# Two cross-attention layers on one core: the first layer's output projection, three of its products in two levels, others among the last weighted rows

## The chip, the cores and the metric

The kernel runs on one core of a Trainium2 chip. The metric is the device time of one execution in microseconds; the median of three runs of the kernel before is 636.7 us. All arithmetic is in 32-bit floating point.

## The reference

Two cross-attention layers, eight batches of 100 query rows with 1024 features, and a context of 1444 rows with 512 features for each batch. Cut to what matters:

```python
# layer 0: scale = 1024 ** -0.5
Q = x @ Wq + bq;  K = ctx @ Wk + bk;  V = ctx @ Wv + bv
weights = softmax(Q @ K.T * scale, axis=keys)
x = x + (weights @ V) @ Wo + bo
# layer 1: its own Wq, bq, Wk, bk, Wv, bv
w = softmax((x @ Wq + bq) @ (ctx @ Wk + bk).T * scale, axis=queries)
x = w @ (ctx @ Wv + bv) + x
out = layernorm(x) * gamma + beta
```

The first layer's softmax runs over the keys of a query, the second layer's over the queries of a key.

## The kernel before

**Weights multiplied first.** The kernel never builds Q, K or V. It multiplies Wq with Wk (`wqk0`, `wqk1`; tiles qk in the trace) and Wv with Wo (`wvo`; tile vo) for itself, and then works with the context's 512 features. For each layer `queries` makes gT = (x Wq Wk)^T for two groups of four batches, 400 columns each (tiles g0T, g1T). For each batch `scores` multiplies gT with the context (L846), the softmax follows, and `weighted_rows` multiplies the weights with the context again (L817, tile A). In the first layer the result is copied to A0T (L830), and `project0` multiplies it with vo and adds it to xT, which holds x transposed as eight blocks of 128 features by 800 columns.

**Seven products for eight.** Large products are done by Winograd's form of Strassen's scheme: four sums of quarters of the left factor (S1 to S4), four of the right (T1 to T4), and seven products X, Z, Y, X again, W, X again, Y again. X and Y are pairs of PSUM banks into which later products accumulate; after every product VectorE adds the bank to the quarters of the result that it belongs to (`add`), or ScalarE copies it (`put`). A bank cannot be accumulated into again before the last add has read it. `seven_products` (L202) does one level. `inner_product` (L255) does one product of the outer scheme by a second level of seven, with half the columns and half the blocks; it writes its own sums over its factors where it can, and yields after each of its seven products.

**Order.** TensorE's instructions stand in the program's order. The other engines' order is set by the framework's scheduler, except that VectorE calls made while `vector.in_order` is set keep their place in the program (L94 to L98; all such calls have line L96 in the profile, all matmuls of the schemes L163). Each engine works through its list in order, and waits at an instruction until what it needs is there.

**Buffers.** `unit` gives one of ten stream buffers, which hold context rows (c), context features (cT) and scratch; `bank` one of six PSUM banks, `bank2` one of two more. A buffer is taken again once its last reader is done. SP's DMA queue issues the context loads in order; GpSimd's queue loads Wv, gamma, beta and bv of the second layer.

**Around the change.** `alternated` runs a batch's 48 weighted-row matmuls (each shows as two instructions), alternating with the scores of the batch two further on; batches 6 and 7 of the first layer have no further scores and run alone. `project0` (L936) yields two `seven_products`, one for each half j of the 1024 output features; the rows r and groups g of the result are the quarters. X and Z of the first half need only the first group; they run between batches 6 and 7:

```python
        if b == B - 1:

            o0 = list(project0(AS, A0))
            next(o0[0])
            next(o0[0])
        run(alternated(b, 0, softmax0, A0[b // G][:, :, b % G * T : (b % G + 1) * T]))
```

After batch 7 come X of the second half, the rest of the first half, the rest of the second, and then the second layer's `queries` (products g_x, g_y, a second-level Z named g_z, g_x, a second-level W named g_w alternating with the last product of X). Meanwhile `key_bias_sums` (L570) makes the second layer's key bias: eight steps over 800 columns (L576, L578; tile kb), each adding to the last, then in `key_biases` a transpose and a reduction, and in `totals` a matmul (L546, tile c), three small VectorE operations, and `key_bias[1]`, which ScalarE adds to the scores when it evicts them (L858). That matmul stands just ahead of the second layer's first scores. Then follow g_y's last product, the scores of batch 1, and the weighted rows of batch 0.

Of the kernel before, what the change touches and what calls it, by code (L numbers as in the profile page):

```python
# [25 lines left out]
F32 = mybir.dt.float32  # L26
# [29 lines left out]
def two_layer_cross_attention(ctx: ExitStack, tc: tile.TileContext, a: dict, out: bass.AP):  # L56
# [23 lines left out]
    def row(name):  # L80
        return work.tile([P, E], F32, tag="row", name=name, bufs=3)
# [98 lines left out]
    def combine(to, x, y, op, engine=vector):  # L180
        for t, p, q in zip(to, x, y):
            engine.tensor_tensor(t, p, q, op)
# [69 lines left out]
        add(0, 1, Y)  # L252
        yield

    def inner_product(name, lhs, rhs, nb, width, t, put, add, right=None):  # L255

        h, w = nb // 2, width // 2

        def quarters(x, n):
            if len(x) == 1:
                return ([x[0][:, 2 * k : 2 * k + 2, c]] for c in halves(n) for k in range(2))
            return ([x[2 * k + i][:, c] for i in range(2)] for c in halves(n) for k in range(2))

        def room(x, t):
            t = t.rearrange("p (i n) -> p i n", i=2)
            return [t] if len(x) == 1 else [t[:, i, :] for i in range(2)]  # L270

        A11, A12, A21, A22 = quarters(lhs, nb * P)
        B11, B21, B12, B22 = quarters(rhs, width)
        S1, T1 = room(lhs, t[:, : 2 * h * P]), room(rhs, t[:, 2 * h * P : 2 * h * P + 2 * w])

        T2, T3, T4 = B11, B12, B21
        if right:
            T1, T2, T3, T4 = right
        combine(S1, A21, A22, ALU.add)
        combine(T1, B12, B11, ALU.subtract)  # L280
        combine(A21, A11, A21, ALU.subtract)
        combine(T3, B22, B12, ALU.subtract)

        def product(ps, left, right, fresh):
            half_product([ps], left, right, fresh, h, w)

        def steps():
            X = bank(f"{name}_x")
            product(X, A11, B11, True)
            put(0, 0, X)  # L290
            combine(T2, B22, T1, ALU.subtract)
            combine(A11, S1, A11, ALU.subtract)
            yield
            Z = bank2(f"{name}_z")
            product(Z, A12, B21, True)
            add(0, 0, Z)
            combine(T4, B21, T2, ALU.subtract)
            combine(A12, A12, A11, ALU.subtract)
            yield
            Y = bank(f"{name}_y")  # L300
            product(Y, S1, T1, True)
            put(1, 1, Y)
            yield
            product(X, A11, T2, False)
            put(0, 1, X)
            yield
            W = bank2(f"{name}_w")
            product(W, A22, T4, True)
            put(1, 0, W)
            yield  # L310
            product(Y, A12, B22, False)
            add(0, 1, Y)
            yield
            product(X, A21, T3, False)
            add(1, 1, X)
            add(1, 0, X)
            yield

        return steps()

    def halves(n):
        return slice(0, n // 2), slice(n // 2, n)
# [217 lines left out]
            tc.keep_in_program_order(ins)  # L540
        nc.vector.tensor_reduce(sums, t.rearrange("p (c q i) -> p c q i", q=P // QD, i=QD), AX.X, ALU.add)

    def totals(name, sums, n):

        ps = bank(name)[:, : n * P // QD]
        nc.tensor.matmul(ps, same, sums.rearrange("p c q -> p (c q)"), start=True, stop=True)  # L546
        own = small.tile([P, 2 * EC, P // QD], F32, tag="own", name=f"{name}_own", bufs=1)[:, :n, :]
        mask = quarter.unsqueeze(1).to_broadcast([P, n, P // QD])
        nc.vector.tensor_tensor(own, ps.rearrange("p (c q) -> p c q", q=P // QD), mask, ALU.mult)
        got = const.tile([P, n], F32, tag=name, name=name)  # L550
        nc.vector.tensor_reduce(got, own, AX.X, ALU.add)
        return got
# [17 lines left out]
    def key_bias_sums(name, wqbk):  # L570

        acc = work.tile([P, B * T + P - T], F32, tag="kb", name=name, bufs=1)
        nc.gpsimd.memset(acc[:, B * T :], 0.0)
        for k in range(EC):
            if k == 0:
                nc.vector.tensor_scalar(acc[:, : B * T], xT[:, k, :], wqbk[:, k : k + 1], None, ALU.mult)  # L576
            else:
                nc.vector.scalar_tensor_tensor(  # L578
                    acc[:, : B * T], xT[:, k, :], wqbk[:, k : k + 1], acc[:, : B * T], ALU.mult, ALU.add
                )  # L580
        return acc

    def key_biases(name, kb, bqbk):

        sums = quarter_sums(name)[:, :B, :]
        t = row(f"{name}_t").rearrange("p (b q j) -> p b q j", q=P // QD, j=QD)

        src = bass.AP(kb.tensor, kb.offset, [list(kb.ap[0]), [T, B], [QD, P // QD], [1, QD]])
        vector.transpose(t, src)
        vector.tensor_reduce(sums, t, AX.X, ALU.add)  # L590
        yield
        c = totals(name, sums, B)
        nc.vector.tensor_scalar(c, c, SCALE, bqbk, ALU.mult, ALU.add)
        yield c

    def queries(layer, w, u, between=None):
# [4 lines left out]
        H, nb, h = EC // 2, 2, GT // 2  # L601
        A11, A12, A21, A22 = ([w[:, k * H : (k + 1) * H, j * 256 : j * 256 + 256]] for j in range(2) for k in range(2))
        B11, B21, B12, B22 = ([xT[:, k * H : (k + 1) * H, g * GT : g * GT + GT]] for g in range(2) for k in range(2))
        S1, S2 = ([row(f"g{layer}_s{n}").rearrange("p (c l) -> p c l", c=H)] for n in (1, 2))
        T1, T2 = ([wide(f"g{layer}_t{n}")] for n in (1, 2))
        T3 = [work.tile([P, LC, GT], F32, tag="gT", name=f"g{layer}_t3", bufs=3)]
        dst = [work.tile([P, LC, GT], F32, tag="gT", name=f"g{layer}T_{g}", bufs=3) for g in range(2)]

        def put(r, g, banks):
            for j in range(2):  # L610
# [25 lines left out]
        def product(banks, lhs, rhs, fresh):  # L636
            half_product(banks, lhs, rhs, fresh, nb, GT)

        t = unit(f"g{layer}_t")

        def inner(n, lhs, rhs, put, add, right=None, at=0):
            return inner_product(f"g{layer}_{n}", lhs, rhs, nb, GT, t[:, at:], put, add, right)
# [3 lines left out]
            return [[t[:, n, :].rearrange("p (i t) -> p i t", i=2)] for n in range(4)]  # L646

        def steps():
            X = pair("x")
            product(X, A11, B11, True)  # L650
            put(0, 0, X)
            yield
            S3, S4 = A21, A12
            if layer == 0:
                Z = pair("z")
                product(Z, A12, B21, True)
            vector.in_order = layer == 0
            combine(S1, A21, A22, ALU.add)
            vector.in_order = True
            combine(T1, B12, B11, ALU.subtract)  # L660
            combine(S2, S1, A11, ALU.subtract)
            if layer == 0:
                combine(T2, B22, T1, ALU.subtract)
                vector.in_order = False
                yield
                vector.in_order = True
                add(0, 0, Z)
            combine(S3, A11, A21, ALU.subtract)
            if layer == 0:
                combine(T3, B22, B12, ALU.subtract)  # L670
            Y = pair("y")
            product(Y, S1, T1, True)
# [22 lines left out]
            V = half_steps(X, S3, T3, False, nb, GT)  # L695
            for n, _ in enumerate(inner("w", A22, T1, *parts(1, 0))):
                next(V)
                if layer == 0 and n == 1:
                    between()
                elif layer == 0 and n == 3:  # L700

                    add(0, 1, Y)
                    _, more = parts(0, 1)
                    Q = inner("q", S4, B22, more, more, four(T2[0]), 768)
# [62 lines left out]
    run(steps)  # L767
    wqbk0 = totals("wqbk0", sums_c, 2 * EC)
    nc.vector.tensor_tensor(out_bias, out_bias, wqbk0[:, EC:], ALU.add)
    kb0 = key_bias_sums("kb0", wqbk0[:, :EC])  # L770
    wqk1, (acc_c, acc_u) = next(qk1)
    c0 = next(got[0])
    for t in prob:
# [161 lines left out]

    def project0(AS, A0):  # L936

        Bs = [[A0[g][:, 2 * k + i, :] for i in range(2)] for g in range(2) for k in range(2)]
        t12, t4 = (work.tile([P, LC, GT], F32, tag="gT", name=f"o0_t{n}", bufs=3) for n in (12, 4))
        T_ = ([t12[:, i, :] for i in range(2)], [t12[:, 2 + i, :] for i in range(2)], Bs[2], chunks(t4, 2))  # L940
        for j, (A, S) in enumerate(AS):

            def add(r, g, banks, j=j):
                e = 4 * j + 2 * r
                add_to_queries([e, e + 1], g * GT, GT, banks)

            right = None if j else (lambda n: right_sums(Bs, T_, (n,)))
            yield seven_products(f"o0_{j}", A, Bs, S, T_, 2, GT, add, add, right=right)


    def softmax1(s, parts):
# [174 lines left out]
    first_transposed(batches[0], 0)  # L1126
    run(steps)
    for b in range(B):
        if b == B - 1:

            o0 = list(project0(AS, A0))
            next(o0[0])
            next(o0[0])
        run(alternated(b, 0, softmax0, A0[b // G][:, :, b % G * T : (b % G + 1) * T]))
        for e in range(2 * b, 2 * b + 2) if 2 * b < EC else ():
            add_out_bias(e)
        if b == 0:
# [3 lines left out]
        if b == 1:  # L1141
# [2 lines left out]
            vector.in_order = True  # L1144
            AS = value_sums(wvo)
            vector.in_order = False
    next(o0[1])
    for steps in o0:
        run(steps)

    gT[1], steps = queries(1, wqk1, u1)
    run(islice(steps, 5))
    kb1 = key_bias_sums("kb1", wqbk1)
    *_, key_bias[1] = key_biases("c1", kb1, bqbk1)
    vectors = [unit(f"vectors_{j}") for j in range(2)]
    gamma, beta = (t[:, :E] for t in vectors)
    bv1 = [t[:, E:] for t in vectors]
# [5 lines left out]
    nc.gpsimd.dma_start(out=wv1, in_=a["L1_xattn_Wv"].rearrange("(c p) e -> p c e", p=P))  # L1163


    run(first_scores(0, 1, softmax1))
    run(steps)
    run(first_scores(1, 1, softmax1))

# [44 lines left out]
```

## Time and profile before

| | |
|---|---|
| median of three runs | 636.7 us (636.08 to 637.99) |
| the profiled execution's own time | 636.75 us |
| its span | 635.0 us |
| TensorE busy, weight loads | 623.8 us, 530.7 us |
| VectorE, ScalarE, GpSimd busy | 472.4, 165.7, 98.7 us |
| granted clock | 0.997 mean |
| batches 6 and 7 with X and Z of the projection between | 322.9 to 350.6 us |
| rest of the projection, twelve products | 350.6 to 382.9 us |
| second layer's queries, up to its first scores | 382.9 to 414.4 us |
| first scores, g_y, second scores | 414.4 to 439.9 us |

An execution's time is its span and 1.75 us around it. A matmul's shown duration overlaps with the next one's start, so the distance from start to start is what it takes of the engine. On VectorE too the next instruction starts before the last one's shown end, unless it needs that result. A row of the timeline is start, duration, engine, line, operation, out<-in, shapes, count, and in brackets the idle time ahead of it and what ended it.

### The profile page before, as it was taken

Reading aid. Unit: us, or ns where it says so; the run is one execution under the profiler, and the core shown is the slowest. Engines: PE = TensorE matmul, PEld = TensorE weight load, DVE = VectorE, ACT = ScalarE, POOL = GpSimd, SP = SyncE. Lnnn points to the kernel's source line nnn. Section 1 sums busy time; section 2 is a strip of 40 time slices with the busy share of each in tenths; the row PEclk is TensorE's granted clock in tenths of the full one; section 3 lists DMA queues with packets and bytes.
Section 4 is the critical chain, followed back from the end, with each engine's and each line's share of the span. In section 5 each row is a group of like instructions: output and inputs, shape, how many; then the busy total and the mean of one; then the engine's idle time right before and its main releaser. Section 6 shows DMA issues by size and latency. Waiting matters only on the chain.

```text
span 635.0 us, 10448 instructions
## 1 busy us (share of the span) xinstructions
PE 623.8 (98%) x4112; PEld 530.7 (84%) x4112; DVE 472.4 (74%) x940; ACT 165.7 (26%) x377; POOL 98.7 (16%) x129
## 2 busy tenths in 40 slices
PE   9999999999999999999999999999999999999994
PEld 8886466688985999999998656756999999999992
DVE  2955779998884797676654789639777659898886
ACT  1522310105204244323230001113433240325301
POOL 2111200002300000000000001007211220544054
PEclk9999999999999999999999999999999999999998
DMA  8989997015779889998965206156899990699002
GB/s 270 298 166 295 307 333 242 1 47 103 154 272 387 277 299 310 334 300 310 310 220 186 91 0 232 48 192 189 284 303 303 320 313 26 196 322 339 30 18 87
DMA packets 51943, 138.32 MB, mean 218 GB/s; under 512 B 4339, under 2 KB 8691, under 8 KB 51895
## 3 DMA queue, kind: packets, MB, share of 16 engines
q1 hardware_dynamic: 46792, 120.85, 55.9%
q0 software_dynamic: 4704, 16.35, 11.3%
q8 instruction: 32, 0.52, 0.3%
q10 hardware_dynamic: 398, 0.47, 0.2%
q14 instruction: 17, 0.13, 0.1%
HBM read 123.36 MB, written 3.28 MB: 199 GB/s over the span
## 4 chain that ended last, share of the span: by engine, by line
PE 92%; DVE 3%; DMA 2%; issue 1%; POOL 1%; POOLq 0%; ACT 0%; DVEq 0%; SPq 0%
PE s L846 25%; PE A L817 25%; PE qk_x L163 7%; PE o_x L163 5%; PE g_x L163 4%; PE o_y L163 3%; PE qk_y L163 2%; PE qk_z L163 2%; PE vo_x L163 2%; DMA vo<-in_L_xattn_Wo 2%; PE g_y L163 2%; PE o_w L163 2%; PE o_z L163 2%; PE qk_w L163 1%; PE vo_y L163 1%; PE z L1045 1%
## 5 line engine op out<-in xcount | busy, mean ns | idle before, releaser
L817 PE MATMUL A<-w,c 120*128 120x100 f32 (+1 forms) x1536 | 247.7, 265 | 0.0
L817 PEld LDWEIGHTS A<-w,c 120*128 120x128 f32 (+1 forms) x1536 | 215.9, 190 | 0.8
L96 DVE STREAM_TRANSPOSE w<-prob 32x384 f32<-32x384 f32 (+1 forms) x256 | 143.7, 561 | 35.1 <-ACT prob L858 15.7
L846 PE MATMUL s<-cT,g1T 128*100 128x131 f32 (+2 forms) x592 | 122.9, 296 | 0.3 <-DVE g1T L96 0.3
L846 PE MATMUL s<-cT,g0T 128*100 128x131 f32 (+2 forms) x592 | 122.7, 296 | 0.0
L846 PEld LDWEIGHTS s<-cT,g1T 128*100 128x100 f32 x592 | 78.3, 167 | 9.3 <-DVE g1T L96 1.2
L846 PEld LDWEIGHTS s<-cT,g0T 128*100 128x100 f32 x592 | 78.2, 167 | 8.4 <-PE c L546 0.4
L858 ACT ACTIVATE prob<-s,c 100x393 f32<-100x393 f32 (+2 forms) x64 | 35.0, 560 | 112.8 <-PE s L846 112.5
L968 ACT ACTIVATE w<-w,negmax 120x100 f32<-120x100 f32 (+1 forms) x96 | 34.8, 364 | 82.3 <-DVE negmax L96 82.3
L878 DVE TENSOR_REDUCE maxima<-prob 100x1 f32<-100x394 f32 (+3 forms) x32 | 16.5, 528 | 24.3 <-ACT prob L858 24.0
L1163 POOL DMA_DIRECT2D wv<-in_L_xattn_Wv x1 | 0.8, 772 | 202.7 <-PE o_x L163 202.7
L163 PE MATMUL qk_x<-qk 128*128 128x256 f32 x128 | 30.4, 386 | 0.0
L987 POOL TENSOR_TENSOR part<-w 120x500 f32<-120x500 f32 x8 | 10.9, 1366 | 113.0 <-DVE rstd L1062 28.6
L163 PEld LDWEIGHTS qk_x<-qk 128*128 128x128 f32 x128 | 23.9, 195 | 3.2 <-ACT qk L413 0.2
L528 POOL DMA_DIRECT2D qk_L_xattn_bk<-qk_L_xattn_bk x8 | 6.9, 863 | 98.1 <-ACT qk_L_xattn_bk L524 80.6
L612 ACT ACTIVATE g1T<-g_x,k 128x400 f32<-128x400 f32 x4 | 2.4, 594 | 69.2 <-PE g_x L163 69.0
L96 DVE TENSOR_TENSOR xT<-xT,o_x 128x400 f32<-128x400 f32 (+1 forms) x32 | 15.8, 539 | 4.5 <-PE o_x L163 4.3
L968 ACT ACTIVATION_READ_ACCUMULATOR w<-w,negmax 120x1 f32 (+1 forms) x96 | 17.9, 186 | 0.0
L1067 POOL TENSOR_TENSOR z<-z,vectors 100x1024 f32<-100x1024 f32 x7 | 16.5, 2358 | 8.2 <-ACT z L1066 8.2
L1066 ACT ACTIVATE z<-z,rstd 100x1024 f32<-100x1024 f32 x7 | 8.0, 1149 | 31.9 <-POOL rstd L1063 31.9
L1045 PE MATMUL z<-ident,xT 128*100 128x128 f32 x64 | 16.3, 273 | 0.0
L96 DVE TENSOR_TENSOR w<-w,rtotal 120x400 f32<-120x400 f32 (+1 forms) x24 | 15.6, 648 | 0.7
(335 smaller groups left out, 965.5 us busy)
## 6 DMA issues: line engine op xcount, KB each, us to landing
cT<-in_ctxT SPq DMA_DIRECT2D x64, 722.0 KB, 6.7
c<-in_ctx SPq DMA_DIRECT2D x48, 768.0 KB, 8.9
c<-in_ctx SPq DMA_DIRECT2D x16, 512.0 KB, 7.5
vo<-in_L_xattn_Wo SPq DMA_DIRECT2D x8, 512.0 KB, 11.0
qk_L_xattn_bk<-qk_L_xattn_bk POOLq DMA_DIRECT2D x8, 512.0 KB, 6.1
qk<-in_L_xattn_WqT SPq DMA_DIRECT2D x8, 512.0 KB
qk<-in_L_xattn_WqT SPq DMA_DIRECT2D x15, 256.0 KB, 5.9
c<-in_ctx SPq DMA_DIRECT2D x16, 224.0 KB, 6.0
```

Of the source, the lines that this page charges most:

```text
L96: ins = getattr(nc.vector, op)(*args, **kw)
L163: nc.tensor.matmul(banks[n // per][:, n % per * width : (n % per + 1) * width], lhs[i][:, n * P : (n + 1) * P], rhs[i], start=(fresh and i ...
L528: nc.gpsimd.dma_start(out=tiles[i], in_=tiles[i + n], accum_op=ALU.add)
L817: nc.tensor.matmul(ps[:, k * T : (k + 1) * T], c[m // CQ][:r, m % CQ, k * P : (k + 1) * P], w[:r, m, :], start=(m == 0 and k == 0), stop=( ...
L846: nc.tensor.matmul(banks[n // per][:T, cuts[n] - o : cuts[n + 1] - o], q[:, k, t0 : t0 + T], cT[k][:, cuts[n] : cuts[n + 1]], start=(k == ...
L858: nc.scalar.activation(p[:, part], ps[:T, : part.stop - part.start], AF.Identity, bias=key_bias[layer][:T, b : b + 1], scale=SCALE,)
L878: nc.vector.tensor_reduce(maxima[:, n : n + 1], p[:, part], AX.X, ALU.max)
L968: nc.scalar.activation(w[:r, m0 + m, :], w[:r, m0 + m, :], AF.Exp, bias=negmax[:r, m : m + 1], accum_out=total[:r, m : m + 1])
L987: add(part, w[:MR, 0:5, :], w[:MR, 5:10, :], ALU.add)
L1045: nc.tensor.transpose(ps[:T, e * P : (e + 1) * P], xT[:, 4 * j + e, b * T : (b + 1) * T], ident)
L1066: nc.scalar.activation(z, z, AF.Copy, scale=rstd)
L1067: nc.gpsimd.tensor_tensor(z, z, beta[:T], ALU.add)
```

## The change

Three products of the projection become second-level ones: Z of the second half ("o0_z1"), W of the second half ("o0_w1") and the last Y product of the second half ("o0_q1"). The other eleven stay. X and Z of the first half are now issued one matmul at a time among batch 6's weighted rows, one after every four; the second-level Z of the second half the same way among batch 7's. All VectorE work of the projection after that is in program order. `inner_product` can take all of its sums ahead of its products (`ahead`), into scratch.

The second layer's `queries` take their first three sums (two into stream buffers) during batch 7 and the fourth in the middle of the projection, and yield within g_w. The eight key-bias steps, in program order now, stand between the yields of g_z, g_x and g_w; the bias's matmul stands ahead of the last two matmuls of batch 0's scores, and takes its bank from `bank2`. The core of the diff:

```diff
@@ inner_product
-        combine(A21, A11, A21, ALU.subtract)
+        combine(S3, A11, A21, ALU.subtract)
         combine(T3, B22, B12, ALU.subtract)
+        if ahead:
+            second()
+            fourth()
...
-            combine(T2, B22, T1, ALU.subtract)
-            combine(A11, S1, A11, ALU.subtract)
+            if not ahead:
+                second()
             yield
...
@@ key_bias_sums
-        for k in range(EC):
-            if k == 0:
-                nc.vector.tensor_scalar(acc[:, : B * T], xT[:, k, :], wqbk[:, k : k + 1], None, ALU.mult)
...
-        return acc
+        def steps():
+            for k in range(EC):
+                if k == 0:
+                    vector.tensor_scalar(to, xT[:, k, :], wqbk[:, k : k + 1], None, ALU.mult)
+                else:
+                    vector.scalar_tensor_tensor(to, xT[:, k, :], wqbk[:, k : k + 1], to, ALU.mult, ALU.add)
+                yield
+
+        return acc, steps()
...
-        c = totals(name, sums, B)
+        c = totals(name, sums, B, bank2)
...
@@ project0
+        (A, S), (A_, S_) = AS
+        X = pair("x")
+
+        def first():
+            yield from half_steps(X, A[0], B11, True, 2, GT)
+            add(0, 0, 0, X)
+            Z = pair("z")
+            yield from half_steps(Z, A[1], B21, True, 2, GT)
+            add(0, 0, 0, Z)
+
+        yield first()
+        vector.in_order = True
+        yield inner("z", 1, 0, 0, A_[1], B21, room[:, :512], right)
+        combine(T1, B12, B11, ALU.subtract)
+        X_ = pair("x")
+        product(X_, A_[0], B11, True)
+        combine(T2, B22, T1, ALU.subtract)
+        add(1, 0, 0, X_)
+        Y = pair("y")
+        product(Y, S[0], T1, True)
+        combine(T4, B21, T2, ALU.subtract)
+        combine(T3, B22, T3, ALU.subtract)
+        add(0, 1, 1, Y)
+        product(X, S[1], T2, False)
+        add(0, 0, 1, X)
+        W = pair("w", bank2)
+        product(W, A[3], T4, True)
+        add(0, 1, 0, W)
+        W = inner("w", 1, 1, 0, A_[3], T4, room[:, 512:])
+        product(X, S[2], T3, False)
+        add(0, 1, 1, X)
+        add(0, 1, 0, X)
+        product(Y, S[3], B22, False)
+        add(0, 0, 1, Y)
+        yield
+
+        Y = pair("y")
+        product(Y, S_[0], T1, True)
+        Q = inner("q", 1, 0, 1, S_[3], B22, room[:, :512], right)
+        add(1, 1, 1, Y)
+        product(X_, S_[1], T2, False)
+        add(1, 0, 1, X_)
+        run(W)
+        add(1, 0, 1, Y)
+        product(X_, S_[2], T3, False)
+        add(1, 1, 1, X_)
+        add(1, 1, 0, X_)
+        run(Q)
+        vector.in_order = False
...
@@ the first layer's loop
+            more = next(o0)
+            if b == B - 1:
+                gT[1], queries1 = queries(1, wqk1, u1)
+            for n, _ in enumerate(steps):
+                if n % 4 == 3 and n > 4:
+                    next(more, None)
+                    if b == B - 1 and n < 16:
+                        next(queries1)
...
-    next(o0[1])
-    for steps in o0:
-        run(steps)
-
-    gT[1], steps = queries(1, wqk1, u1)
-    run(islice(steps, 5))
-    kb1 = key_bias_sums("kb1", wqbk1)
-    *_, key_bias[1] = key_biases("c1", kb1, bqbk1)
+    next(o0)
+    next(queries1)
+    run(o0)
+
+    kb1, more = key_bias_sums("kb1", wqbk1)
+    steps = queries1
+    for n, _ in enumerate(islice(steps, 5 + 7)):
+        if n > 2:
+            vector.in_order = True
+            next(more, None)
+    run(more)
+    biases1 = key_biases("c1", kb1, bqbk1)
+    next(biases1)
+    vector.in_order = False
...
-    run(first_scores(0, 1, softmax1))
+    scores1 = first_scores(0, 1, softmax1)
+    run(islice(scores1, LC * NB - 2))
+    key_bias[1] = next(biases1)
+    run(scores1)
     run(steps)
```

On VectorE's list this gives, from the end of batch 7's rows: the first half's right sums and adds as the products end; the eight sums of o0_w1 ahead of X's last adds; the second layer's 1600-column sum and the eight sums of o0_q1 ahead of the second half's Y adds; o0_w1's eight adds; the four adds of X's last product, and behind them the eight adds of o0_q1. In g_w one key-bias step stands ahead of the two last g_w_x adds and one behind them, ahead of the four adds of g_x.

## The prediction

> **What bounds the kernel now.** The page's first part first: TensorE's share says whether anything but matmul time can count.
>
> ```profile
> PE 623.8 (98%) x4112; PEld 530.7 (84%) x4112; DVE 472.4 (74%) x940; ACT 165.7 (26%) x377; POOL 98.7 (16%) x129
> ```
>
> TensorE is idle for 11.2 of 635.0 us. The table of windows says how much of that lies where the change works (PE, PEld, DVE, ACT, POOL, clock, DMA share):
>
> ```profile
> 350.80:362.00 11.20, 11.20 (x34) 6.31 (x34) 9.72 (x18) 0.00 (x0) 0.00 (x0) 1.00 0.26 96
> ...
> 372.00:382.40 10.40, 10.40 (x32) 5.88 (x32) 8.90 (x14) 0.00 (x0) 1.42 (x3) 1.00 0.06 6
> 382.40:396.00 13.60, 13.50 (x47) 8.24 (x46) 13.33 (x18) 2.37 (x4) 1.49 (x3) 1.00 0.67 266
> 396.00:415.60 19.60, 19.27 (x80) 13.88 (x80) 12.74 (x27) 2.90 (x6) 0.00 (x0) 1.00 0.12 39
> ```
>
> The projection runs on TensorE without a hole, with VectorE 86% busy or more beside it, then full. Third, TensorE's timeline, for prices and small holes:
>
> ```profile
> 337.24 2.85 PE L163 MATMUL o_z<-A0T,vo 128*128 128x400 f32 x8
> 339.93 10.86 PE L817 MATMUL A<-w,c 120*128 120x100 f32 x96
> 350.63 2.88 PE L163 MATMUL o_x<-A0T,vo 128*128 128x400 f32 x8
> 353.34 2.85 PE L163 MATMUL o_y<-o_t,o_s 128*128 128x400 f32 x8
> ...
> 394.99 0.84 PE L163 MATMUL g_z_y<-g_t,g_t 128*128 128x200 f32 x4
> 395.93 0.94 PE L163 MATMUL g_z_x<-g_t,qk 128*128 128x200 f32 x4
> ...
> 414.31 0.30 PE L546 MATMUL c<-c_sums,same 128*128 128x32 f32 x2
> 414.44 0.83 PE L846 MATMUL s<-cT,g1T 128*100 128x361 f32 x2
> 415.61 9.37 PE L846 MATMUL s<-cT,g1T 128*100 128x361 f32 x30 [0.34 <-DVE g1T L96]
> ```
>
> Starts count, since durations overlap. A projection product takes 339.93 - 337.24 = 2.69 (eight instructions), 2.71 behind weighted rows. Two holes belong to before: g_z_x and g_z_w start 0.45 late together (four of 128x200 take 0.675), and the second score piece 0.56 late (415.61 for 414.44 + 0.61). VectorE and ScalarE beside the second hole:
>
> ```profile
> 411.88 0.36 DVE L96 TENSOR_TENSOR g1T<-g1T,g_w_y 128x200 f32<-128x200 f32 x1 [4.21 <-PE g_w_y L163]
> 413.16 0.63 DVE L96 TENSOR_TENSOR g1T<-g1T,g_w_x 128x200 f32<-128x200 f32 x2 [0.92 <-PE g_w_x L163]
> 413.83 2.21 DVE L96 TENSOR_TENSOR g1T<-g1T,g_x 128x400 f32<-128x400 f32 x4
> ...
> 423.19 2.39 ACT L858 ACTIVATE prob<-s,c 100x361 f32<-100x361 f32 x4 [12.30 <-PE s L846]
> ```
>
> The third add of the four ends at 415.55 and frees x's first bank; the piece starts 0.06 later.
>
> **Prices** (start to start): add or sum of 400 columns 0.485, of 200 0.275, of 128 0.20, of 1600 1.74; a key-bias step 0.97, chained 1.08. VectorE follows a matmul's next start by about 0.19; TensorE follows VectorE's end by 0.05.
>
> **Matmuls.** Three products of 2.69 become fourteen instructions of 0.169 (g_w rows) = 2.36: 3 x 0.33 = 0.98 saved. The alternation moves X, Z and the split Z into the weighted rows. These run at 10.70 / 96 = 0.111 each, alone or not, so nothing is saved; each switch to a projection matmul may cost the 0.02 seen at 350.63. Thirteen more switches: 0 to 0.26; I take 0.26, the only row there is.
>
> **Moved at no cost.** The three layer-1 weight sums (1.14 each) and the split Z's sums and adds (1.9 + 2.2) go under batch 7's rows, where VectorE idled 10.1; uncovered they cost up to 7.5. SP's queue keeps its order, but three more stream buffers are taken ahead: batch 6's rows load one buffer later, batch 7's three. They were issued by 312 and 322 and are used from 323 and 340; the last quarter of batch 7 now waits for batch 6's first quarter (about 326), lands 9 later and is wanted near 349. GpSimd's list keeps its order; its Wv load waits for the last read of vo, at 380 as before.
>
> **VectorE's fixed order in the projection.** Let 0 be TensorE's first matmul after batch 7's rows. A prime marks the second output half, a figure the product's turn in its banks; products follow at 2.69: Y2 ends 16.1, Y' 18.8, X'2 21.5, the split W begins there. VectorE: Y2's second add starts 16.3, the layer-1 sum of 1600 columns 16.9, the split Y's eight sums 18.7 (4 x 0.20 + 4 x 0.275), Y' and X'2 adds 20.6 (4 x 0.485), so W's first add starts 22.5 and ends 22.86. The fourth W matmul must not accumulate before that read: wanted at 22.5, it starts 22.9. **Stall 0.4** (0 if VectorE is 0.5 earlier, 0.9 if 0.5 later). Queued behind it are all later adds.
>
> Then X'3 runs 24.3 to 26.9, and its four adds stand ahead of the split Y's first add: 26.5 and 27.1 (as its banks finish), 27.6, 28.1; the split's add starts 28.6 and ends 28.95. Its fourth matmul, wanted at 27.95, starts 29.0. **Stall 1.05** (0.7 to 1.2). Before, the whole product there waited only for adds long done.
>
> **Layer-1 queries.** With the key-bias steps gone, VectorE reaches g_z's first add 0.2 sooner (it was 0.2 late at 394.70): 0 to 0.45 back, I take 0.1, since the chain add, 400-column sum, 256-column sum to g_z_x remains.
>
> **Scores.** The eight steps move into the 4.2 idle before 411.88, but do not fit: from the second 1600-column sum on, VectorE runs without pause. One step precedes the two g_w_x adds, one follows. Relative to TensorE's last g_x matmul, the first x add starts 1.4 later than before (two steps, 2 x 0.97, less the 0.5 it had to wait). The c matmul no longer takes a bank, so the third score piece, not the second, needs x's first bank: wanted at +1.22, it starts at +2.50. **Stall 1.28 for 0.56: +0.72** (-0.56 if VectorE keeps up, +1.3 if the second piece still needs that bank).
>
> **The key bias.** c now stands before the last two score matmuls. From c to a ready bias: 0.30 + 0.66 (the three small ops at 415.96 to 416.62) + latencies = 1.04. The rest of the scores is 1.36, so ScalarE's first eviction starts 0.33 before their end instead of 1.63 (423.19 against 424.82). Four at 0.44 end 1.55 after it; before 0.76. The transposes and softmax are 0.79 later; the scaled rows were ready at 439.50 and used at 439.93, 0.38 to spare with the latency. **Stall 0.41** (0 to 0.9).
>
> **Sum:** -0.98 + 0.26 + 0.4 + 1.05 - 0.1 + 0.72 + 0.41 = +1.76 on the profiled 636.75 (span 635.0 and 1.75 around it): **638.5**. The median of the runs is 636.7. Laying out before's own order by these prices gives holes of 0.18 and 0.54 for 0.45 and 0.56, and VectorE's starts within 0.35.
>
> **Rules weighed.** The add rows say that two halves cost 0.55 where a whole cost 0.485, and a split product has eight adds where a whole one has two: 24 x 0.275 - 6 x 0.485 = 3.7 us more VectorE, all in the layout above. [...]
>
> The windows hold the clock at 1.00 even where TensorE was idle 1.5 of 14 us (52 to 66). [...]
>
> **Rivals.**
> *Weight loads hidden, not slower (0.07).* If wide matmuls let loads run several ahead, batch 6 with X and Z would fall to its matmul time, 96 x 0.085 (half of 0.169) + 16 x 0.336 = 13.5 for 16.1, and batch 7 with split Z to its loads, 110 x 0.111 = 12.2 for 13.1: 3.5 off, 635.0. It decides if a weighted-row matmul beside a projection goes below 0.111. Against it: qk_w's eight 128-column matmuls take 0.89 both among 256-column ones and alone.
> *VectorE keeps up (0.16).* If sums and adds queue 1 us less, the split stalls fall to 0.1 together and the score hole to 0.2: 638.5 - 1.35 - 1.1 = 636.0, no change. Against it: VectorE's windows are full already, and the four X'3 adds wait for their product.
> *VectorE falls behind (0.20), slower.* A backlog of another 1.2 us when X'3's adds begin (waits on its own results, dearer small sums) passes to the split Y, the scores and the softmax, which has no slack left: 1.2 to 1.8 more, 640.0.
>
> **Numbers.** The forecast itself has 0.57, with 637.4 to 639.4 as its own range. The range, 635.6 to 640.2, takes in most of the other cases. Differences under 0.3% (1.9 us) can hardly be told from none here; 638.6 is that edge, so the forecast is split 0.30 slower, 0.27 the same. Slower: 0.30 + 0.18 of the last rival; faster (under 634.8): 0.05, the first rival with a stall gone too; the rest is within 0.3%.
>
> **What would show it.** Each term: split products at 2.36; a hole of about 1 us at the fourth matmul of the split Y, released by VectorE; one above 1 us at the third score piece; the first layer-1 weighted row late, released by VectorE; key-bias steps between g1T adds. It is wrong if TensorE is dense through the splits, or if the score hole is gone.

## The result, and the profile after

The changed kernel takes 640.49 us (median of four runs, 640.25 to 641.22) against 636.49 us (four runs of the kernel before on the same chip): a ratio of 1.0054, 95% interval 1.0040 to 1.0067. It is slower. The prediction said slower or the same and gave 638.5 us, so the direction was right. The time lies 0.3 us above the upper end of its range, 640.2; as a ratio to the kernel before, 1.0054, it falls just short of that end (640.2 / 636.7 = 1.0055). What was missed is a piece of work some 220 us ahead of the stage the change is about.

TensorE's share in the page of the kernel after is the same 98%, with 18 TensorE instructions (nine matmuls) and 44 VectorE instructions more:

```profile
PE 624.3 (98%) x4130; PEld 533.4 (84%) x4130; DVE 481.6 (75%) x984; ACT 165.1 (26%) x377; POOL 98.8 (15%) x129
```

The waits of TensorE in the kernel after (what waited, for whom: us in total, times, longest) are where the reading starts:

```profile
PE vo_z L163 <- DMA vo<-in_L_xattn_Wo: 1.6, 1, 1.6
PE warm L108 <- DVE ones L105: 1.1, 1, 1.1
PE s L884 <- DVE g1T L96: 1.0, 1, 1.0
PE vo_q_x L163 <- DVE vo L96: 0.9, 1, 0.9
PE o_q_x L163 <- DVE xT L96: 0.9, 1, 0.9
PE o_w_x L163 <- DVE xT L96: 0.2, 1, 0.2
```

The first two were there before, and the score wait was 0.3. Two of the new waits, o_q_x and o_w_x, are the holes that were predicted in the split products. The third, vo_q_x, is new and was not predicted at all: it is in the product of Wv with Wo for the first layer, near 99 us.

Cutting both profiled executions at the same TensorE instructions gives the ledger (us; each figure is the distance between two starts in the timeline, the last column is the span):

| | to vo_y | to u | to batch 6 | to first g_x | to second g_x | to second g_y | to layer 1's first weighted row | to the end | span |
|---|---|---|---|---|---|---|---|---|---|
| before | 69.17 | 32.69 | 221.08 | 59.95 | 15.93 | 26.00 | 15.11 | 195.07 | 635.0 |
| after | 69.62 | 34.12 | 221.05 | 60.81 | 15.82 | 26.63 | 15.10 | 195.15 | 638.3 |
| difference | +0.45 | +1.43 | -0.03 | +0.86 | -0.11 | +0.63 | -0.01 | +0.08 | +3.3 |

The cut called "batch 6" is made at the first weighted row behind the last alternated score; in all traces the last four matmuls of batch 5 stand behind that cut.

The first column is the arrival of the first weights and scatters: in the twelve profiled executions of this study it lies between 68.37 and 70.96, with no relation to the kernel that these twelve show. The stages that the prediction was about, the four from batch 6 to the first weighted row, cost 1.37 together where 1.76 was predicted. The largest single piece, 1.43, stands in the column "to u". Around the span the four runs after spend 1.95 to 3.02 us, the runs of the kernel before 1.72 to 1.85.

TensorE's timeline of the kernel after, at the places whose rows before were shown:

```profile
327.45 0.86 PE L163 MATMUL o_x<-A0T,vo 128*128 128x400 f32 x2
328.14 1.03 PE L855 MATMUL A<-w,c 120*128 120x100 f32 x8
...
376.39 0.50 PE L163 MATMUL o_w_x<-o_t,vo 128*128 128x200 f32 x2
...
377.81 0.61 PE L163 MATMUL o_w_x<-o_t 128*128 128x200 f32 x2 [0.24 <-DVE xT L96]
...
384.08 0.61 PE L163 MATMUL o_q_x<-o_t,o_t 128*128 128x200 f32 x2 [0.88 <-DVE xT L96]
...
416.90 1.38 PE L884 MATMUL s<-cT,g1T 128*100 128x361 f32 x4
419.25 7.54 PE L884 MATMUL s<-cT,g1T 128*100 128x361 f32 x24 [0.97 <-DVE g1T L96]
```

A projection matmul among weighted rows (two instructions) takes 0.69, the eight rows after it 0.87 (the next pair starts at 329.01): together 1.56, just 2 x 0.336 + 8 x 0.111. The fourth matmul of W starts 1.42 after the first where 1.01 would be dense (0.41 lost), that of the split Y 2.06 after its first at 382.02 (1.05 lost), and the third score piece 2.35 after the first where 1.22 would be dense (1.13 lost). VectorE's rows at the split Y: the four adds of X' come first, and the fourth matmul starts 0.06 after the end of the add behind them.

```profile
381.55 2.20 DVE L96 TENSOR_TENSOR xT<-xT,o_x 128x400 f32<-128x400 f32 x4 [0.42 <-PE o_x L163]
383.67 0.35 DVE L96 TENSOR_TENSOR xT<-xT,o_q_x 128x200 f32<-128x200 f32 x1
```

Now the unforeseen wait. TensorE's row in the kernel after:

```profile
99.97 1.13 PE L163 MATMUL vo_q_x<-vo 128*128 128x256 f32 x4 [0.95 <-DVE vo L96]
```

The product before it starts at 97.99 and takes 0.86 where nothing waits, so vo_q_x is 1.12 late; it and the two products after it take 0.97 each instead of 0.86, and that makes up the rest of the 1.43 (1.44 by these rows).

VectorE's timeline in the kernel before, then in the kernel after, in the same place:

```profile
92.60 0.69 DVE L541 TENSOR_REDUCE u_sums<-qk_L_xattn_bq 128x16 f32<-128x512 f32 x1
95.61 0.41 DVE L96 TENSOR_TENSOR vo<-vo,vo_w_y 128x256 f32<-128x256 f32 x1
97.60 0.48 DVE L96 TENSOR_TENSOR vo<-vo_t,vo 128x128 f32<-128x128 f32 x2
...
105.50 1.82 DVE L96 TENSOR_TENSOR g_t<-xT 128x1600 f32<-128x1600 f32 x1
```

```profile
92.94 1.78 DVE L96 TENSOR_TENSOR g_t<-xT 128x1600 f32<-128x1600 f32 x1
94.65 0.67 DVE L560 TENSOR_REDUCE u_sums<-qk_L_xattn_bq 128x16 f32<-128x512 f32 x1
97.64 0.41 DVE L96 TENSOR_TENSOR vo<-vo,vo_w_y 128x256 f32<-128x256 f32 x1
99.63 0.48 DVE L96 TENSOR_TENSOR vo<-vo_t,vo 128x128 f32<-128x128 f32 x2
```

The first row of the second block is the first layer's query sum T1, 1600 columns wide. In the kernel before it runs at 105.50, after everything that belongs to vo. Now it stands in front of the adds and sums on which vo_q_x depends, and everything behind it is 1.6 us later against TensorE. Its companion, the sum S1 of 1024 columns, moved from 104.36 to 72.98, which cost nothing there.

The reason is one line of the change that the prediction passed over. In the layer-0 branch of `queries`, S1 had been issued with `vector.in_order` set; in the changed kernel the flag is set one line later. S1 thereby lost its fixed place, and the scheduler put both S1 and the T1 behind it ahead of work that TensorE needs sooner. T1 itself is issued under the flag in both kernels and moved all the same, so "keeps its place in the program" is not the whole rule for a flagged call; why T1 could follow S1 ahead of vo's adds, no trace shows.

```diff
-            vector.in_order = layer == 0
-            combine(S1, A21, A22, ALU.add)
+                combine(S1, A21, A22, ALU.add)
             vector.in_order = True
```

### The profile page after: what moved, and what is told of

It is laid out like the page before. It is cut to its first block, busy times and chain, and to the rows that moved or that the text cites. A ratio compares the mean times of both kernels' runs of the same rounds, so it can differ in the third digit from the quotient of the medians.

```text
span 638.3 us, 10536 instructions
## 1 busy us (share of the span) xinstructions
PE 624.3 (98%) x4130; PEld 533.4 (84%) x4130; DVE 481.6 (75%) x984; ACT 165.1 (26%) x377; POOL 98.8 (15%) x129
## 4 chain that ended last, share of the span: by engine, by line
PE 91%; DVE 4%; DMA 2%; issue 1%; POOL 1%; POOLq 0%; ACT 0%; DVEq 0%; SPq 0%
PE s L884 25%; PE A L855 24%; PE qk_x L163 7%; PE g_x L163 5%; PE o_x L163 4%; PE g_y L163 3%; DMA vo<-in_L_xattn_Wo 2%; PE o_y L163 2%; PE qk_z L163 2%; PE qk_y L163 2%; PE vo_x L163 1%; PE o_z L163 1%; PE o_w L163 1%; DVE vo L96 1%; PE qk_w L163 1%; PE vo_y L163 1%
## 5 line engine op out<-in xcount | busy, mean ns | idle before, releaser
L1150 DVE SCALAR_TENSOR_TENSOR z<-vectors,r,z 100x512 f32<-100x512 f32 x16 | 11.8, 740 | 4.9 <-PE z L1146 4.8
```

What stands on the lines that cost most here:

```text
L1150: nc.vector.scalar_tensor_tensor(z[:, half], bv1[j][:T], s["r"], ps[:T, :], ALU.mult, ALU.add)
```

## The experiments

All were timed against the kernel before on their own chip; its medians there were 636.67 (first four runs), 637.11 (the next four) and 637.25 (the last two).

**The layer-0 sums.** First the one line put back in the changed kernel:

```diff
                 product(Z, A12, B21, True)
+                vector.in_order = True
                 combine(S1, A21, A22, ALU.add)
```

> The changed kernel with one line put back: the first layer-0 query sum (1024 columns) is again held in VectorE's program order, so that it and the 1600-column sum behind it stay after the last add of the vo product. Theory (hoisted sum): the two sums had slid up into the vo product; the 1600-column one ran at 92.9, ahead of the adds for which the vo_q products wait, and cost TensorE 1.43 us there. Expected: no wait of vo_q_x for VectorE, batch 6's weighted rows about 1.4 earlier, 639.1 us, against 640.49 for the change. Rival (arrival of the first weights): the 1.85 us by which batch 6 started late are the loads' own scatter from run to run; then vo_q_x still starts when its operands allow, and the time stays at 640.3 to 640.6.

Measured: 639.09 us (ratio to before 1.0042, 1.0030 to 1.0054), 1.40 less than the median of the change. By the ratios to the kernel before, 1.0042 and 1.0054, it is 0.8, and the two intervals overlap, so the times alone do not show the gain; the trace does. The column "to u" is back at 32.69, and the wait of vo_q_x is gone. All other columns but the first stay within 0.1 of the change.

Then the reverse, the kernel before with only that line changed:

> The kernel before with that one line alone changed: the first layer-0 query sum is no longer held in VectorE's program order, and nothing of the projection is touched. Theory (hoisted sum): 1.4 us slower than before, 637.9 against 636.5, with a wait of about 0.9 us of vo_q_x for VectorE near 98 us and everything behind it later by the same 1.4. Rival (arrival of the first weights): no change, 636.5.

Measured: 638.71 us, ratio 1.0031 (1.0019 to 1.0043), 2.04 more than before where 1.4 was expected; but the column "to u" is 34.12, exactly that of the change, and the rest equals the kernel before within 0.1 except for the arrival of the first weights (69.77). The waits of TensorE in this run hold the same new line:

```profile
PE vo_q_x L163 <- DVE vo L96: 1.0, 1, 1.0
```

Put in or taken out, the line is worth 1.43 us in the trace: in the ten traces with S1 in fixed order the column is 32.68 or 32.69, in the two without it 34.12. The rival, scatter of the loads, accounts for the 0.45 of the first column and no more.

**The score hole.**

```diff
         if n > 2:
             vector.in_order = True
+        if 2 < n < 9:
             next(more, None)
```

> The changed kernel with the line put back and the last two of the eight key-bias steps moved behind the four x adds (six steps before, two after). Theory (two steps of 0.97 hold up the third x add, which frees the bank of the third score piece): the hole of 1.13 us falls to 0.1 (0 to 0.3), since the third add then ends about 1.7 after the first g_x bank is done; 638.1 us against 639.1 with the line alone put back. The bias sums end 4 us before the c matmul as it is, so nothing waits for the moved steps. Rival (the x adds are late because of the g_w_x adds ahead of them or because the second piece waits too): a hole of 0.5 or more stays and the gain is under 0.6.

Measured: 638.23 us, ratio 1.0024 (1.0015 to 1.0033). The pieces now run without a hole:

```profile
415.74 8.85 PE L885 MATMUL s<-cT,g1T 128*100 128x361 f32 x28
```

From the first piece to g_y it takes 10.10 instead of 11.15, so 1.05 came back, as expected, and the column "to second g_y" is 25.59, 0.41 better than before. The two key-bias steps ahead of the third add were all of this hole.

**The split products.** Three of the split Y's adds ahead of the second pair of X' adds:

```diff
         add(1, 1, 1, X_)
+        run(islice(Q, 3))
         add(1, 1, 0, X_)
```

> The changed kernel with the line put back and the first three adds of the split Y product moved ahead of the second pair of X' adds on VectorE. Theory (the fourth matmul of the split waits behind four adds of 0.485): the split falls from 3.58 to 2.5 to 2.7 us; 638.1 us against 639.1. Rival (the wait is for the products' own ends or for the sums, not for the queue): the split stays above 3.2. A third outcome: the later X' adds free their banks 1 us later, and the hole comes back in the layer-1 queries.

Measured: 638.95 us, ratio 1.0036 (1.0024 to 1.0048), and only 0.08 came back in "to first g_x" (60.74). The fourth matmul is only 0.08 late, but the last product waits:

```profile
383.92 0.61 PE L163 MATMUL o_q_x<-o_t,o_s 128*128 128x200 f32 x2 [0.63 <-DVE xT L96]
```

It accumulates into the same bank, so it needs the fourth add, which still stood behind the two X' adds. The expectation had named only the fourth matmul, and missed by 0.8 for it. With four adds ahead:

> The changed kernel with the layer-0 line put back and the first four adds of the split Y, in place of three, moved ahead of the second pair of X' adds. With three, the wait went from the fourth matmul to the last one, which needs the fourth add: 0.63 of it was left. Theory (the queue ahead of these adds is all there is to it): the split takes 2.4 to 2.6 us in place of 3.58, and the time is 638.1 against 639.1. Rival (VectorE is short of time whatever the order): the wait moves on to g_x or to the layer-1 queries and less than 0.3 us comes back there.

Measured: 638.11 us, ratio 1.0019 (1.0008 to 1.0029); "to first g_x" is 59.84, so 0.98 came back, and nothing was given back later. The split Y takes 2.61. The next run takes 1.74 us of VectorE's backlog away and leaves the order of the adds as it is:

```diff
     next(o0)
-    next(queries1)
     run(o0)
+    vector.in_order = True
+    next(queries1)
```

> The changed kernel with the layer-0 line put back and the first layer-1 sum of 1600 columns moved behind the whole projection, into VectorE's idle 4.7 us before the g_y product. Theory (that sum of 1.74 us is the backlog that makes W's first add late, while the split Y waits for four adds tied to their own product): W's hole of 0.40 goes, the split Y keeps 0.9 to 1.05, and the first g_y starts unhindered; 638.6 against 639.1. Rival (the backlog is all one): both holes go and 1.5 us come back. Against both: the sum is then late for g_y, and a hole appears there.

Measured: 638.66 us, ratio 1.0024 (1.0014 to 1.0034). W's first to fourth start is 1.10 instead of 1.42; the split Y's stays 2.06. "To first g_x" is 60.48, 0.34 better; g_y did not wait. So W's hole is backlog (0.08 of it is left), and the split Y's is the order of one queue: 1.74 us less work ahead of it changes nothing.

Both products whole again:

```diff
-        run(W)
-        add(1, 0, 1, Y)
+        W = pair("w", bank2)
+        product(W, A_[3], T4, True)
+        add(1, 1, 0, W)
...
-        run(Q)
+        product(Y, S_[3], B22, False)
+        add(1, 0, 1, Y)
```

> The changed kernel with the layer-0 line put back, and W and the second Y of the second output half as whole products of eight matmuls again; Z stays split, the alternation stays. Theory (each split saves 0.33 of matmuls and costs a stall behind VectorE's queue: 0.58 and 1.22 us by the two traces): the whole pair takes 2 x 2.69 = 5.38 in place of 2.94 + 3.58 = 6.52; from batch 6's first weighted row to the first g_x 59.7 us in place of 60.8, and 638.0 us against 639.1. Rival (the stalls are VectorE's backlog, whatever the product's form): the whole products wait as well, and under 0.4 us comes back.

Measured: 637.26 us, ratio 1.0000 (0.9989 to 1.0011). "To first g_x" is 59.66: 1.16 came back, and against before 0.29 is gained. That is the split Z among batch 7's rows, 0.33, less what the switches cost (0.03, below). The time is 0.7 under the 638.0 expected, though the trace gave back what was expected (1.16 for 1.1); part of that is the time around the span, 1.83 in the mean here and 2.31 in the run with the line alone put back.

**The key bias.** The c matmul behind the last score matmul:

```diff
-    run(islice(scores1, LC * NB - 2))
+    run(islice(scores1, LC * NB))
...
-                if (k, n) != (LC - 1, n_pieces - 1):
+                if (k, n) != (LC - 1, n_pieces - 1) or (layer, b) == (1, 0):
```

> The changed kernel with the layer-0 line put back and the key bias's c matmul moved once more, from before the last two pairs of score matmuls to behind the last. ScalarE's first eviction then starts 1.28 later against TensorE, VectorE's first multiply of scaled rows as well. In the change the first weighted row of layer 1 was not late at all, where 0.41 was predicted. Theory (that multiply waits until GpSimd's running instruction has ended: it ended 0.44 after it in all four rows of the two traces): the delay of the change was absorbed, this one is not: the multiply falls into the last of GpSimd's sums, takes about 0.97, and the weighted row is 1.5 late. Rival (the multiply's length has nothing to do with GpSimd, and the row had 0.4 more slack than reckoned): it takes 0.57 and the row is 1.1 late or less. 640.2 to 640.6 us.

Measured: 640.21 us, ratio 1.0053 (1.0035 to 1.0072). The first weighted row is 0.99 late (16.09 instead of 15.10 behind g_y), and the multiply took 0.69. The multiply's length falls between the two expectations, 0.97 and 0.57; the row's delay lies within what the rival allowed (1.1 or less). The row starts at 443.13, 0.09 behind the multiply's end; the profile names no releaser for this wait (0.74, "issue"). The next part shows that the wait for GpSimd is real all the same, and why the expected size was wrong.

The rows of the scaling multiply on VectorE and of the pair of GpSimd sums beside it: before, after, and this run, in that order.

```profile
437.99 1.51 DVE L96 TENSOR_TENSOR w<-w,rtotal 120x400 f32<-120x400 f32 x1
439.62 1.44 DVE L96 TENSOR_TENSOR w<-w,rtotal 120x400 f32<-120x400 f32 x1
437.80 2.82 POOL L182 TENSOR_TENSOR wv_s<-wv,wv_s 128x512 f32<-128x512 f32 x2
```

```profile
442.07 0.68 DVE L96 TENSOR_TENSOR w<-w,rtotal 120x400 f32<-120x400 f32 x1
443.52 0.79 DVE L96 TENSOR_TENSOR w<-w,rtotal 120x400 f32<-120x400 f32 x1
441.05 2.83 POOL L182 TENSOR_TENSOR wv_s<-wv,wv_s 128x512 f32<-128x512 f32 x2
```

```profile
442.35 0.69 DVE L96 TENSOR_TENSOR w<-w,rtotal 120x400 f32<-120x400 f32 x1
440.10 2.50 POOL L182 TENSOR_TENSOR wv_s<-wv,wv_s 128x512 f32<-128x512 f32 x2
```

Before, the second GpSimd sum ends at 440.62 and the second multiply at 441.06; after, 443.88 and 444.31; here 442.60 and 443.04. The first sum of the pair takes 1.26: it ends at 439.06 and the first multiply at 439.50; after, at 442.31 and 442.75. In all five the multiply ends 0.43 to 0.44 behind the end of the GpSimd instruction that was running when it began, whatever its own start; with GpSimd idle it takes 0.57 (the one at 443.79 here). The traces with the line alone put back and with four adds ahead hold two such multiplies each; all nine end 0.42 to 0.44 behind. No run moved or removed the GpSimd sums alone. The second sum of a pair is stretched from 1.27 to 1.59 or 1.60 where a multiply came in ahead of it. In this run none did, so the sum ended 0.33 earlier than I had reckoned from the change, and the multiply waited for less. The rest of the miss is slack: after the change the multiply ended 0.40 ahead of the row, here 0.09, and the expectation had counted on next to none.

**Put together.** The four repairs in one kernel, then the version with W and Y whole:

> The changed kernel with four edits together: the layer-0 line put back, the 1600-column layer-1 sum behind the projection, four of the split Y's adds ahead of the second pair of X' adds, and the last two key-bias steps behind the x adds. Theory (the four losses lie in different places and add up): against the line alone put back 0.33 + 0.98 + 1.05 = 2.4 us come back, so 636.7 against 639.1, and from the kernel before it differs by -0.5 in the projection, -0.1 in the queries and -0.4 in the scores: 1.0 us faster than before, 0.16%. Rival (the orders share VectorE's time, so that one gain eats another: the moved sum meets the late X' adds and is late for g_y): under 1.7 us come back and the kernel is no faster than before.

Measured: 636.96 us against 637.25, ratio 0.9997 (0.9986 to 1.0008): no difference that can be told, and 1.0 was expected. In the trace the terms do add up: "to first g_x" 59.52, the queries 15.82, the scores 25.58, together 0.96 less than before, and the waits of TensorE name VectorE no more, but for the first instruction. The spans of its runs have a median of 634.45 against 635.50, but around the span they spend 2.01 in place of 1.77 (in the mean 2.22 in place of 1.78).

> The changed kernel with the layer-0 line put back, W and the second Y of the second half whole, and the last two key-bias steps behind the x adds: the alternation, the split Z and the moved bias sums are left of the change. Theory (terms add up): -0.3 in the projection, -0.1 in the queries, -0.4 in the scores against before, 0.8 us faster than before; 0.2 slower than the run with both splits in a better order. Rival: whole products give VectorE so much time that the rest of the queue moves too and it is the faster of the two.

Measured: 636.58 us, ratio 0.9986 (0.9974 to 0.9998). The interval just leaves out 1, the only one of ten that does so on the faster side: by 0.67 us in the medians this version beats the kernel before, if only just. Its trace gains 0.81 in the three stages, as expected. It was expected to be 0.2 slower than the combined one, and is not: its stages are 0.15 longer, but the time around its span is 1.82 in the mean, near that of the kernel before, where the combined one spends 2.22. The spans of the two, 634.79 and 634.90 in the mean, can't be told apart.

In the combined kernel, where nothing queues any more, one thing is still to be seen in the split W (TensorE, then the weight loads):

```profile
375.67 0.61 PE L163 MATMUL o_w_x<-o_t 128*128 128x200 f32 x2
376.12 0.50 PE L163 MATMUL o_w_w<-o_t,vo 128*128 128x200 f32 x2
376.45 0.57 PE L163 MATMUL o_w_y<-o_t,o_t 128*128 128x200 f32 x2
376.86 0.50 PE L163 MATMUL o_w_x<-o_t,vo 128*128 128x200 f32 x2
```

```profile
375.67 0.30 PEld L163 LDWEIGHTS o_w_x<-o_t 128*128 128x128 f32 x2 [0.23 <-DVE xT L96]
```

The pair that accumulates into the first bank starts 0.08 late and takes 0.45 where others take 0.34, since its weight load waits for VectorE together with it and starts when it does, where the loads of the pairs on either side start 0.17 ahead of theirs; the second turn in Y's bank takes 0.41. Together 0.26; what holds up the second turn in Y's bank, the profile does not name. A second-level product of this width between whole products thus takes 2.62 even in the best order tried, against 2.69 whole: it saves 0.07, not 0.33.

## Why the prediction was right or wrong

**The missing term.** The step that failed is the list of moved work, "Moved at no cost" and "VectorE's fixed order in the projection". It followed every instruction from batch 6 on and took all before that for unchanged. The layer-0 sums belong in that list: 1.43 us by the trace of both runs that undid and did that line alone; their times (1.40 and 2.04 by the medians, 0.8 and 2.0 by the ratios) scatter around it. Added to the prediction's sum it gives 639.9. The profiled execution took 3.50 more than before's where 1.76 was forecast: 1.43 for the missing term, 0.45 for the first weights, 0.20 around the span and 0.05 elsewhere, less 0.39 by which the four stages came out smaller (key bias 0.42, switches 0.23 and scores 0.09 less, the splits 0.36 more). That errors of both signs met here, so that the total missed by less than the missing term and the scatter together, is luck.

**Matmuls.** Three times 0.33: right for matmuls alone (Z shows it in full), but W and Y lose 0.18 each beside the hole itself: 0.11 where a weight load comes out of hiding, 0.07 at the second turn in Y's bank. The prediction had no such term.

**Switches**, +0.26 predicted: 0.03 (by the rows there are fourteen more of them, not thirteen). From batch 6's first weighted row to the second half's X it takes 30.08; before it took 27.69, and the split Z adds 2.36. The 0.02 seen at 350.63 before is not paid at a switch among the rows.

**W's hole**, 0.4: 0.41, and with the unhidden load and the second turn 0.58. **The split Y's hole**, 1.05: 1.05, with both 1.22. The mechanism was right to the instruction: four adds ahead in the queue. **Queries**, -0.1: -0.11. **Scores**, +0.72: +0.63 (a hole of 1.13, where 1.28 was laid out).

**The key bias**, +0.41: zero. Against TensorE (3.22 later there) the multiply does start 0.86 later, as reckoned (0.79). But the 1.51 of its row before was not its length: 0.94 of it was a wait for GpSimd. Starting later, it waited less, and ended at 439.53 of before's time instead of 439.50. The run with c later still shows the slack: 1.28 more delay cost 0.99.

In the kernels before and after, the sum that was running when the first multiply began took 1.26, as the sums with no multiply beside them do, and the multiply ended 0.44 behind it. Why the multiply waits was not shown.

**Add prices and the clock.** Adds of 200 columns in the split Y start 0.28 apart (384.13, 384.41), as the price of 0.275 has it; the durations shown for them, 0.36 and 0.35, overlap. The window of the kernel after with both split holes keeps the clock at 1.00 (the column after GpSimd's), with TensorE idle for 1.12 of 14 us:

```profile
372.00:386.00 14.00, 12.88 (x52) 8.77 (x51) 13.20 (x34) 0.00 (x0) 2.91 (x5) 1.00 0.10 31
```

**The rivals.** Weight loads hidden: no, each block of a projection matmul and eight rows takes the sum of its parts (1.56). VectorE keeps up: no, both split holes came. (The argument against it, that VectorE's windows are full, was too strong: in the window 362 to 372 us, which the prediction's table leaves out, VectorE was busy for 7.81 of 10.00 us.) VectorE falls behind: no; the time it gave, 640.0, was nearly met, but for another reason, and the backlog touches W alone.

## What to carry to other kernels

Compare every engine's whole instruction list of the two kernels, from the first instruction, not only the stage that the diff speaks of: a flag moved by one line changed an order 220 us earlier and cost more than any term that was worked out. Where products are split, each add that frees a bank belongs in the queue ahead of any work not needed yet (four adds put ahead brought 0.98 back); the weight load of the matmul that waits for it came out of hiding here (0.11); with the late start (0.08) and the second turn in Y's bank (0.07) that ate 0.26 of the 0.33 saved. A long row is not always a long instruction (1.51 here, against 0.57 with GpSimd idle): compare it with the same instruction elsewhere before its length is used as a price.

## What was not expected of the hardware

A VectorE multiply of 120 x 400 with both inputs in SBUF took 0.57 with GpSimd idle and up to 1.51 beside its sums, and in all nine rows that began beside one it ended 0.42 to 0.44 behind the running GpSimd instruction.

The time around the span is 1.72 to 1.85 us in every run of the kernel before, and its median is 1.81 to 1.84 in the three other kernels with W and Y whole (10448 instructions in the kernel before). In the eight kernels with both split (10536 in the kernel after) the medians are 1.91 to 2.46 and single runs reach 3.58. What makes this was not tried and stays open. It makes 0.40 of the 0.51 (means) by which the combined kernel, 0.15 shorter in its stages, is slower than the version with W and Y whole and the key-bias steps moved.
